# The first block's edges from the 49th on, held in the last block's tiles of a graph network

## The chip, the cores and the metric

The kernel runs on one core of one Trainium2 chip. The time is the device time of one execution in microseconds (us), and the smaller it is the better.

## The reference, cut to what matters

A graph has 6,250 nodes and 206,250 edges, sorted by their destination node; each node has an edge to itself, which stands last among its edges. The program is a two-part graph network.

```
h = relu(layernorm(x))
x = x + L0(h)                 # per edge: relu([h[dst], ea16] @ W1 + b1), mean over the edges of a node
h = relu(layernorm(x))
x = x + L1(h)                 # three attention layers, h -> h -> h
# one attention layer:
q, k, v = h @ Wq + bq, h @ Wk + bk, h @ Wv + bv
e       = ea32 @ We                                   # per edge
alpha   = sum(q[dst] * (k[src] + e)) / sqrt(C)        # per edge and head
a       = softmax of alpha over the edges of one dst
out     = sum over the edges of a * (v[src] + e), + h @ Ws + bs
```

Nodes have between 15 and 58 edges here, 33 on average. All floats are 32 bits wide.

## The kernel before, in words

**Blocks.** The nodes are sorted by their number of edges and cut into 49 blocks of 128, one node to a partition. Block 0 holds the 128 nodes with the most edges, block 48 the 106 with the fewest and 22 empty places. Block `b` has `CAP[b]` tiles: 66 for block 0, 46 for block 1, then fewer and fewer, 24 for block 47 and 22 for block 48; 1,661 in all. Tile `j` of a block holds the `j`-th edge of each of its 128 nodes. The last tile of a block is the edge of the node to itself; it needs no gather. So each attention layer gathers 1,661 - 49 = 1,612 tiles. In block 0 few nodes have more than 48 edges. There `lanes` cuts the gather of tile 48 to the first 64 partitions and that of tiles 49 to 64 to the first 32 (`CAP0`), and the rest of those chunks is zeroed on VectorE (L638).

**Before the layers (L97 to L383).** VectorE and TensorE count the edges of each node, put each node into a class by that number (`CLS` = 31 classes), rank the nodes (`oh`, `cnt`, `cum`, `at`: six VectorE operations over 31 x 49 columns, L275 to L292), and turn the rank into a block (`half[:, 0]`) and a partition (`half[:, 1]`). Checks on the input are summed into `bad`. `layer0` does L0 and gathers the source of each edge into `src[0]`, block by block. Then all engines branch (L397) on the sum of `bad`: at zero the three calls of `attention` follow, otherwise `general`, a path for any graph.

**One attention layer (`attention`).** The tiles of a block are held in chunks of `CT` = 8. `fetch(b)` issues on GpSimd's queue one indirect DMA per tile (`pick`, L447), which reads for each partition the key and value row of one source node from a table in HBM, `tab[l]`, into the tile's slot of a chunk `kv`. The chunks are a ring of 15 buffers in the first attention layer and of 18 in the other two. `load(b)` brings the edges' attributes on SyncE's queue. `process(b)` makes two passes over the chunks on VectorE. In the first, for each chunk, it adds the edge part that TensorE made (`pe`, L688, and L691 for the last tile), multiplies with `q` (L694) and sums (L695); in the first attention layer it also copies the source numbers out of the chunk (L687, a CAST), for the two later layers to use (`src[1]`). Then come the softmax (L701 to L712), with `lack` pushing absent edges down, and a second pass that weights (L717) and sums (L721) each chunk and sets its buffer free. At the end of a block its new rows go through TensorE and are written to the next layer's table (L738 to L740); the last layer instead keeps the block's result `hn` for a scatter on GpSimd's queue (`put`, L453).

**Order.** Blocks run from 0 to 48, with the gathers of a block issued while the one before it is processed:

```
load(0)
fetch(0)
for b in range(NB):
    if b + 1 < NB:
        load(b + 1)
        fetch(b + 1)
    put(b - 2)
    process(b)
put(NB - 2)
put(NB - 1)
```

Each queue runs in its own order. GpSimd's gathers stand in the order of the program. Within VectorE a scheduler mixes the instructions of neighbouring blocks at build time, and the chip runs them strictly in that order. A layer's first gather needs the whole table of the layer before it.

Of the kernel before, what the change touches and what calls it, by code (L numbers as in the profile page):

```python
# [22 lines left out]
F32 = mybir.dt.float32  # L23
# [4 lines left out]
OP = mybir.AluOpType  # L28
# [3 lines left out]
P = 128  # L32
N, E, D = 6250, 206250, 64
NB = 49
# [23 lines left out]
assert len(CAP) == len(LEAST) == NB  # L58
MAXC = max(CAP)

CAP0 = {64: 48, 32: 49}

LOW, HIGH = 20, (CAP0[64], CAP0[32])
CLS = HIGH[0] - LOW + 1 + len(HIGH)
LOOK = RUN + SG * (MAXC + 1) + 3
RMAX = (EP - LOOK) // RUN
assert CAP[1] < HIGH[0] and LEAST[-2] > LOW and RMAX * RUN + LOOK - 1 >= E
# [9 lines left out]

G = 4
NG = NCH // G


def lanes(b, j):

    return min([p for p in CAP0 if b == 0 and j >= CAP0[p]], default=P)


def runs(values):
# [10 lines left out]
def gnn_kernel(ctx: ExitStack, tc: tile.TileContext, x, src_t, dst_t, dst_row, ea16, ea32, eaT16, eaT32, w, out):  # L98
# [15 lines left out]
    with tc.tile_pool(name="chk", bufs=1) as p, tc.tile_pool(name="chk2", bufs=2) as p2, \  # L114
# [36 lines left out]
        def iota(n, mult, pattern=None):  # L151
# [14 lines left out]
        cap = p.tile([P, NB], F32, name="cap")  # L166
# [4 lines left out]
        nc.gpsimd.tensor_copy(cap, k.cap)  # L171
        nc.gpsimd.memset(cap[64:, 0:1], float(CAP0[64]))
        nc.gpsimd.memset(cap[32:64, 0:1], float(CAP0[32]))
# [94 lines left out]
        nc.vector.tensor_scalar(cls, deg, float(LOW), float(HIGH[0]), op0=OP.max, op1=OP.min)  # L268
        for h in HIGH:
            nc.vector.scalar_tensor_tensor(cls, deg, float(h), cls, op0=OP.is_gt, op1=OP.add)  # L270
        nc.vector.tensor_scalar(cls, cls, -float(LOW), float(CLS - 1), op0=OP.add, op1=OP.min)


# [23 lines left out]
        nc.vector.tensor_single_scalar(half_i[:, 1], int_i, P - 1, op=OP.bitwise_and)  # L297
        half = p.tile([P, 2, NB], F32, name="half")
        nc.vector.tensor_copy(half, half_i)
        pperm = pp.tile([P, 4, NB], F32, name="pperm", tag="pc")  # L300
        for b0 in range(0, NB, 7):
            to = p2.tile([P, 7, P], F16, name="to")
# [65 lines left out]
        nc.vector.tensor_tensor(no[:, 0], k.deg, cap, op=OP.is_gt)  # L368
        nc.vector.tensor_tensor(no[:, 1], k.deg, least, op=OP.is_lt)
        nc.vector.tensor_reduce(bad[:, 1:3], no, axis=AX.X, op=OP.add)  # L370
        for b in range(NB):
# [32 lines left out]
class Kept:  # L404
# [5 lines left out]
    def __enter__(self):  # L410
        self.stack = ExitStack()
        tc = self.tc
        cp = self.stack.enter_context(tc.tile_pool(name="kept", bufs=1))
        dr = self.stack.enter_context(tc.tile_pool(name="kdram", bufs=1, space=bass.MemoryType.DRAM))
        t = lambda name, shape, dt=F32: cp.tile([P] + shape, dt, name=name)

        self.num, self.deg, self.cap, self.ends = (t(n, [NB]) for n in ("num", "deg", "cap", "ends"))
        self.num_i, self.at_i = t("num_i", [NB], I32), t("at_i", [NB], I32)
        self.full = t("full", [WOFF[NB]])
        self.lack = t("lack", [WOFF[NB]])  # L420
        self.x1 = t("x1", [NB, D])
# [24 lines left out]
def pick(nc, out, table, idx):  # L446
    return nc.gpsimd.indirect_dma_start(out=out, out_offset=None, in_=table,  # L447
                                        in_offset=bass.IndirectOffsetOnAxis(ap=idx, axis=0))
# [12 lines left out]
def layer0(tc, ea16, ea32, ident, tabx, srcs, k):  # L461
    nc = tc.nc
    with tc.tile_pool(name="g0", bufs=4) as gp, tc.tile_pool(name="e0", bufs=2) as ep, \
# [124 lines left out]
        def put(b):  # L588
            scatter_rows(tc, k, k.tab[0][:, :], k.num_i[:, b:b + 1], k.rows[:, b, 2 * D:], NP - 1)
# [25 lines left out]
                    wait += [(r, b) for r in range(first[g], first[g] + FIN0[g])]  # L615
        for r, _ in wait:
            put(r)


def attention(tc, l, out, ident, slope, k):  # L620
# [5 lines left out]
    with tc.tile_pool(name=f"g{l + 1}", bufs=2) as gp, tc.tile_pool(name=f"e{l + 1}", bufs=3) as ep, \  # L626
# [7 lines left out]
        def fetch(b):  # L634
            for t0, n in chunks[b]:
                kv = kvs[b, t0] = ep.tile([P, CT, KV], F32, name="kv", bufs=15 if l == 0 else 18)
                if lanes(b, t0 + n - 1) < P:
                    nc.vector.memset(kv, 0.0)  # L638
                for j in range(n):
                    o = OFF[b] + t0 + j  # L640
                    if o + 1 < OFF[b + 1]:
                        r = lanes(b, t0 + j)
                        pick(nc, kv[:r, j, :], k.tab[l][:, :], idx[:r, o:o + 1])

        def load(b):
            g = slice(GOFF[b] * P, GOFF[b + 1] * P)
# [18 lines left out]
        def process(b):  # L665
# [12 lines left out]
            for t0, n in chunks[b]:  # L678
                kv = kvs[b, t0]
                pe = pp.tile([P, CT, D], F32, name="pe")  # L680
                for g in range(-(-n // 4)):
                    nc.tensor.matmul(pe[:, 4 * g:4 * g + 4].rearrange("p j f -> p (j f)"), ea[:, t0 // 4 + g, :],  # L682
                                     k.wblk[l], start=True, stop=True)
                m = n - (t0 + n == c)
                if m:
                    if l == 0:
                        nc.vector.tensor_copy(k.src[1][:, OFF[b] + t0:OFF[b] + t0 + m], kv[:, :m, 2 * D])  # L687
                    nc.vector.tensor_add(pair(kv[:, :m, :2 * D]), pair(kv[:, :m, :2 * D]),  # L688
                                         pe[:, :m, None, :].to_broadcast([P, m, 2, D]))
# [4 lines left out]
                nc.vector.tensor_mul(prod[:, :n], kv[:, :n, :D], q[:, None, :].to_broadcast([P, n, D]))  # L694
                nc.vector.tensor_reduce(al[:, :H, t0:t0 + n].rearrange("p h j -> p j h"),  # L695
                                        prod[:, :n].rearrange("p j (h c) -> p j h c", h=H), axis=AX.X, op=OP.add)
# [60 lines left out]
        put(NB - 2)  # L757
        put(NB - 1)


@with_exitstack
# [543 lines left out]
```

## Time and profile before

| | |
|---|---|
| time, median of 3 runs | 6730.41 us (6730.25 to 6735.94) |
| the profiled execution's own time | 6732.95 us |
| its span, first to last instruction | 6731.2 us |
| GpSimd (POOL) busy | 4927.7 us, 73% |
| VectorE (DVE) busy | 3127.9 us, 46% |
| TensorE (PE) busy | 1914.8 us, 28% |
| gathers of attention (L447, `kv<-tab,src`) | 4836, 943 ns each |
| first gather of the three attention layers | at 577.8, 2609.2 and 4639.6 us |

The trace gives each instruction's start and length. A row of a group reads: line, engine, operation, what it writes and reads, how many; then the busy time in us and the mean of one in ns; then the idle time of the engine just before those instructions and what ended it ("issue" where the profile shows no wait). A row of the timeline reads: start, length, engine, line, operation, and in brackets the idle time before it. For a DMA issued from GpSimd, the busy time is that of GpSimd, not that of the transfer.

### The profile page before, as it was taken

The page shows a single profiled execution, that of the slowest core. Times are in us where ns is not written, and L with a number is a line of the kernel's source. Part 1 is how long each engine was busy: PE and PEld are TensorE (multiplying, and loading weights), DVE is VectorE, ACT ScalarE, POOL GpSimd, SP SyncE. Part 2 cuts the span into 40 slices and gives each one's busy share as a digit, 9 for nine tenths or more (in the row PEclk, how much of TensorE's full clock was granted, in tenths as well). Part 3 has the DMA queues.
Part 4 walks back from the last instruction along what each step waited for, and adds up shares of the span by engine and source line. Part 5 has one row for each costly group of instructions (what it writes and reads, how often), then busy time and mean ns, then how long its engine had stood idle before and what let it go on. Part 6 is the DMA issues. An engine that isn't in the chain of part 4 may idle for free. (4 is left out here: it accounts for less than half of the span.)

```text
span 6731.2 us, 26890 instructions
## 1 busy us (share of the span) xinstructions
PE 1914.8 (28%) x4808; PEld 1135.6 (17%) x4808; DVE 3127.9 (46%) x5986; ACT 345.5 (5%) x998; POOL 4927.7 (73%) x5264
## 2 busy tenths in 40 slices
PE   4663232333333332222222222222222222222221
PEld 3442111111111111111111111111111111111110
DVE  7763444444444444444444444444444344444444
ACT  3110000000000000000000000000000000000000
POOL 4556777777777776777777777776777777777776
PEclk9765555555555555555555555555555555555555
DMA  4553232333232322222222222222222222222221
GB/s 144 183 175 122 81 87 79 84 84 84 82 87 81 84 82 60 67 69 66 68 69 68 68 70 67 69 68 64 64 63 68 63 66 66 66 64 67 63 65 55
DMA packets 227799, 535.37 MB, mean 80 GB/s; under 512 B 90199, under 2 KB 106685, under 8 KB 226519
## 3 DMA queue, kind: packets, MB, share of 16 engines
q0 software_dynamic: 172736, 374.78, 19.6%
q1 hardware_dynamic: 52790, 156.27, 7.0%
q10 hardware_dynamic: 2090, 2.48, 0.1%
q14 instruction: 142, 1.16, 0.1%
q8 instruction: 41, 0.67, 0.0%
HBM read 459.32 MB, written 73.87 MB: 79 GB/s over the span
## 5 line engine op out<-in xcount | busy, mean ns | idle before, releaser
L447 POOL DMA_INDIRECT kv<-tab,src x4836 | 4561.7, 943 | 1518.6 <-issue 1410.4
L688 DVE TENSOR_TENSOR kv<-kv,pe 128x1024 f32<-128x1024 f32 (+6 forms) x669 | 745.0, 1114 | 2321.1 <-DMA kv<-tab,src 2152.6
L682 PE MATMUL pe<-wblk,ea 128*128 128x256 f32 x1736 | 901.4, 669 | 3046.8 <-DVE kv L688 2747.1
L682 PEld LDWEIGHTS pe<-wblk,ea 128*128 128x128 f32 x1736 | 505.7, 323 | 3420.6 <-DVE kv L688 2967.0
L682 PE MATMUL pe<-wblk,eaT 128*128 128x256 f32 x868 | 451.4, 668 | 1224.9 <-DVE kv L688 1160.8
L721 DVE TENSOR_REDUCE some<-kv 128x64 f32<-128x512 f32 (+6 forms) x690 | 610.6, 922 | 0.1
L687 DVE CAST src<-kv 128x8 int32<-128x8 f32 (+5 forms) x223 | 41.0, 184 | 1092.5 <-DMA kv<-tab,src 1041.6
L682 PEld LDWEIGHTS pe<-wblk,eaT 128*128 128x128 f32 x868 | 252.1, 322 | 1383.1 <-DVE kv L688 1273.3
L694 DVE TENSOR_TENSOR prod<-kv,more 128x512 f32<-128x512 f32 (+6 forms) x690 | 423.7, 628 | 0.8
L695 DVE TENSOR_REDUCE al<-prod 128x16 f32<-128x512 f32 (+8 forms) x690 | 422.9, 627 | 0.7
L717 DVE TENSOR_TENSOR kv<-kv,more 128x512 f32<-128x512 f32 (+6 forms) x690 | 416.7, 627 | 0.0
L706 ACT ACTIVATE more<-al,m 128x33 f32<-128x33 f32 (+22 forms) x245 | 71.7, 293 | 3189.0 <-DVE m L704 3185.8
L518 PE MATMUL pm<-w0blk,eT 64*128 64x256 f32 x868 | 192.2, 564 | 37.0 <-DVE msg L521 20.0
L659 PE MATMUL turn<-ident,ea 128*128 128x128 f32 x434 | 124.9, 432 | 77.5 <-ACT eaT L660 70.8
L453 POOL DMA_INDIRECT tab<-rows,num_i x49 | 54.5, 1112 | 117.5 <-ACT rows L586 97.9
L539 DVE TENSOR_TENSOR msg<-msg 128x960 f32<-128x960 f32 (+19 forms) x224 | 137.4, 617 | 0.8
L518 PEld LDWEIGHTS pm<-w0blk,eT 64*128 64x128 f32 x868 | 120.3, 276 | 89.6 <-DVE msg L521 25.7
L521 DVE TENSOR_TENSOR msg<-pm,rx 128x1024 f32<-128x1024 f32 x76 | 92.8, 1221 | 77.4 <-PE pm L518 72.0
L447 POOL DMA_INDIRECT e<-in_ea_dram,at_i x98 | 103.8, 1059 | 33.8 <-issue 22.2
L738 PE MATMUL po<-ws,ht 65*128 65x256 f32 x196 | 109.2, 661 | 11.5 <-ACT ht L736 11.5
L674 ACT COPY more<-rows 128x64 f32<-128x64 f32 x147 | 31.6, 216 | 1516.3 <-DVE kv L717 1507.9
L659 PEld LDWEIGHTS turn<-ident,ea 128*128 128x128 f32 x434 | 80.2, 217 | 139.1 <-ACT eaT L660 125.9
(183 smaller groups left out, 1442.8 us busy)
## 6 DMA issues: line engine op xcount, KB each, us to landing
kv<-tab,src POOLq DMA_INDIRECT x4836, 2.5
ea<-eat SPq DMA_DIRECT2D x26, 576.0 KB
ea<-eat SPq DMA_DIRECT2D x24, 512.0 KB
ea<-eat SPq DMA_DIRECT2D x16, 640.0 KB
ean<-e SPq DMA_DIRECT2D x13, 576.0 KB
ea<-ean SPq DMA_DIRECT2D x13, 576.0 KB
eat<-eaT SPq DMA_DIRECT2D x13, 576.0 KB
ea<-eat SPq DMA_DIRECT2D x16, 448.0 KB
```

The source lines that it names most:

```text
L447: return nc.gpsimd.indirect_dma_start(out=out, out_offset=None, in_=table, in_offset=bass.IndirectOffsetOnAxis(ap=idx, axis=0))
L518: nc.tensor.matmul(pm[:, r, u].rearrange("p j f -> p (j f)"), eT[h, t0 // 8 + u, :], k.w0blk[h, :], start=True, stop=True)
L521: nc.vector.tensor_tensor(msg[:, t0:t0 + 16], pm.rearrange("p r u j f -> p (r u j) f"), nega[:, None, :].to_broadcast([P, 16, D]), op=OP.max)
L539: nc.vector.tensor_add(to, msg[:, :h], msg[:, c - h:c])
L659: nc.tensor.transpose(ps[:, i - i0, :], t[:, i, :], ident)
L682: nc.tensor.matmul(pe[:, 4 * g:4 * g + 4].rearrange("p j f -> p (j f)"), ea[:, t0 // 4 + g, :], k.wblk[l], start=True, stop=True)
L688: nc.vector.tensor_add(pair(kv[:, :m, :2 * D]), pair(kv[:, :m, :2 * D]), pe[:, :m, None, :].to_broadcast([P, m, 2, D]))
L694: nc.vector.tensor_mul(prod[:, :n], kv[:, :n, :D], q[:, None, :].to_broadcast([P, n, D]))
L695: nc.vector.tensor_reduce(al[:, :H, t0:t0 + n].rearrange("p h j -> p j h"), prod[:, :n].rearrange("p j (h c) -> p j h c", h=H), axis=AX.X, ...
L717: nc.vector.tensor_mul(v.rearrange("p j (h c) -> p j h c", h=H), v.rearrange("p j (h c) -> p j h c", h=H), ex[:, :H, t0:t0 + n].rearrange( ...
L721: nc.vector.tensor_reduce(some[:, i, :], v.rearrange("p j f -> p f j"), axis=AX.X, op=OP.add)
L738: nc.tensor.matmul(po, ht[:, :P], k.ws[l + 1], start=True, stop=True)
```

## The change

Block 0 keeps gathers for its own tiles 0 to 48 only (`OWN0` = 49). What a node of block 0 has beyond 49 edges is put into places of block 48's tiles that its node there does not use: tile `t` of block 0, from 49 to 64, lies in tile 69 - `t` of block 48 (`SHARE`). For this the nodes of block 48 stand in reverse order on the partitions (`turned`), so that the nodes with the most edges in block 0 meet the empty places and the nodes with the fewest edges in block 48. `share` writes the source numbers of those edges into block 48's part of `src[0]` once, after `layer0`. In `process(0)` the addition of the edge part reads these rows out of block 48's chunks, in reverse order of tiles, and writes them into block 0's own chunks. Block 48's tiles must then be there when block 0 is processed: the two come first in `order`, and block 47 is the last.

The classes become 33 (one for empty places, and the two above 49 in place of 48 and 49), a check that each pair of nodes fits is added to `bad`, and `lanes`, the zeroing of chunks and the tile `cap` go.

```diff
-CAP0 = {64: 48, 32: 49}
-LOW, HIGH = 20, (CAP0[64], CAP0[32])
-CLS = HIGH[0] - LOW + 1 + len(HIGH)
+OWN0 = 49
+SHARE = OWN0 + CAP[-1] - 2
+NOVER = CAP[0] - 1 - OWN0
+LOW, HIGH = 20, (OWN0, OWN0 + 1)
+CLS = HIGH[0] - LOW + 2 + len(HIGH)
...
+        nc.vector.scalar_tensor_tensor(cls, deg, 0.0, cls, op0=OP.is_gt, op1=OP.add)
...
+        turned = p.tile([P, NB], F32, name="turned")
+        nc.vector.tensor_scalar(turned, half[:, 1], -2.0, float(P - 1), op0=OP.mult, op1=OP.add)
+        nc.vector.scalar_tensor_tensor(turned, half[:, 0], float(NB - 1), turned, op0=OP.is_equal, op1=OP.mult)
+        nc.vector.tensor_add(half[:, 1], half[:, 1], turned)
...
+        over = p.tile([P, 2], F32, name="over")
...
+        nc.vector.tensor_scalar(k.over, col[:, OWN0:CAP[0] - 1], k.deg[:, 0:1], None, op0=OP.is_lt)
...
+def share(nc, k):
+    a = k.src[0][:, OFF[0] + OWN0:OFF[0] + CAP[0] - 1]
+    b = k.src[0][:, OFF[NB - 1]:OFF[NB]][:, SHARE - OWN0:SHARE - (CAP[0] - 1):-1]
+    d = k.shared
+    nc.vector.tensor_sub(d, a, b)
+    nc.vector.tensor_mul(d, d, k.over)
+    nc.vector.tensor_add(b, b, d)
...
         def fetch(b):
             for t0, n in chunks[b]:
                 kv = kvs[b, t0] = ep.tile([P, CT, KV], F32, name="kv", bufs=15 if l == 0 else 18)
-                if lanes(b, t0 + n - 1) < P:
-                    nc.vector.memset(kv, 0.0)
-                for j in range(n):
+                for j in range(own_tiles(b, t0, n)):
                     o = OFF[b] + t0 + j
-                    if o + 1 < OFF[b + 1]:
-                        r = lanes(b, t0 + j)
-                        pick(nc, kv[:r, j, :], k.tab[l][:, :], idx[:r, o:o + 1])
+                    pick(nc, kv[:, j, :], k.tab[l][:, :], idx[:, o:o + 1])
+
+        def own_tiles(b, t0, n):
+            return max(0, min(n, (OWN0 if b == 0 else CAP[b] - 1) - t0))
+
+        def shared(t0, n):
+            out, t = [], max(t0, OWN0)
+            while t < min(t0 + n, CAP[0] - 1):
+                c, i = divmod(SHARE - t, CT)
+                u = min(t0 + n, CAP[0] - 1, t + i + 1)
+                out.append((t - t0, u - t0, kvs[NB - 1, c * CT][:, i - (u - t) + 1:i + 1, :2 * D][:, ::-1]))
+                t = u
+            return out
...
-                m = n - (t0 + n == c)
+                m = own_tiles(b, t0, n)
...
-                if m < n:
-                    nc.vector.tensor_add(pair(kv[:, m:n, :2 * D]), pair(own[:, None, 2 * D:4 * D]),
-                                         pe[:, m:n, None, :].to_broadcast([P, 1, 2, D]))
+                for i, j, rows in shared(t0, n) if b == 0 else []:
+                    nc.vector.tensor_add(pair(kv[:, i:j, :2 * D]), pair(rows),
+                                         pe[:, i:j, None, :].to_broadcast([P, j - i, 2, D]))
+                if t0 + n == c:
+                    nc.vector.tensor_add(pair(kv[:, n - 1:n, :2 * D]), pair(own[:, None, 2 * D:4 * D]),
+                                         pe[:, n - 1:n, None, :].to_broadcast([P, 1, 2, D]))
...
-        load(0)
-        fetch(0)
-        for b in range(NB):
-            if b + 1 < NB:
-                load(b + 1)
-                fetch(b + 1)
-            put(b - 2)
+        order = [0, NB - 1] + list(range(1, NB - 1))
+        for b in order[:2]:
+            load(b)
+            fetch(b)
+        for i, b in enumerate(order):
+            if i and i + 1 < NB:
+                load(order[i + 1])
+            if i and i + 1 < NB:
+                fetch(order[i + 1])
+            if i > 1:
+                put(order[i - 2])
             process(b)
-        put(NB - 2)
-        put(NB - 1)
+        put(order[-2])
+        put(order[-1])
```

More of the change, by code (lines that the diff above doesn't have):

```diff
@@ L79 @@
 NG = NCH // G
-def lanes(b, j):
-    return min([p for p in CAP0 if b == 0 and j >= CAP0[p]], default=P)
 def runs(values):
@@ L165, in gnn_kernel @@
                                 pattern=[[1, P]], channel_multiplier=-1)
-        cap = p.tile([P, NB], F32, name="cap")
         least = p.tile([P, NB], F32, name="least")
@@ L170, in gnn_kernel @@
                 nc.gpsimd.memset(t[:, i:j], float(v))
-        nc.gpsimd.tensor_copy(cap, k.cap)
-        nc.gpsimd.memset(cap[64:, 0:1], float(CAP0[64]))
-        nc.gpsimd.memset(cap[32:64, 0:1], float(CAP0[32]))
         going = p.tile([P, CLS, NB], BF16, name="going")
@@ L367, in gnn_kernel @@
         no = p.tile([P, 2, NB], F32, name="no")
-        nc.vector.tensor_tensor(no[:, 0], k.deg, cap, op=OP.is_gt)
+        nc.vector.tensor_tensor(no[:, 0], k.deg, k.cap, op=OP.is_gt)
         nc.vector.tensor_tensor(no[:, 1], k.deg, least, op=OP.is_lt)
         nc.vector.tensor_reduce(bad[:, 1:3], no, axis=AX.X, op=OP.add)
+        over = p.tile([P, 2], F32, name="over")
+        nc.vector.tensor_scalar(over[:, 0:1], k.deg[:, 0:1], float(CAP[0] - 1), -float(OWN0), op0=OP.min, op1=OP.add)
+        nc.vector.tensor_scalar(over[:, 1:2], k.deg[:, NB - 1:], float(CAP[-1] - 1), None, op0=OP.min)
+        nc.vector.tensor_add(over[:, 1:2], over[:, 1:2], over[:, 0:1])
+        nc.vector.tensor_scalar(over[:, 1:2], over[:, 1:2], float(CAP[-1] - 1), None, op0=OP.is_gt)
+        nc.vector.scalar_tensor_tensor(bad[:, 4:5], over[:, 0:1], 0.0, over[:, 1:2], op0=OP.is_gt, op1=OP.mult)
+        nc.vector.tensor_scalar(k.over, col[:, OWN0:CAP[0] - 1], k.deg[:, 0:1], None, op0=OP.is_lt)
         for b in range(NB):
@@ L420, in __enter__ @@
         self.lack = t("lack", [WOFF[NB]])
+        self.over = t("over", [NOVER])
+        self.shared = t("shared", [NOVER])
         self.x1 = t("x1", [NB, D])
@@ L617, in layer0 @@
             put(r)
+        share(nc, k)
+def share(nc, k):
[5 more added lines that the diff above has]
+    nc.vector.tensor_add(b, b, d)
 def attention(tc, l, out, ident, slope, k):
```

## The prediction

> **What bounds the kernel now.** I read the page first, then the groups, then GpSimd's waits and its timeline over 577 to 720 us and around the two changes of layer, then VectorE's timeline there.
>
> ```profile
> PE 1914.8 (28%) x4808; PEld 1135.6 (17%) x4808; DVE 3127.9 (46%) x5986; ACT 345.5 (5%) x998; POOL 4927.7 (73%) x5264
> L447 POOL DMA_INDIRECT kv<-tab,src x4836 | 4561.7, 943 | 1518.6 <-issue 1410.4
> POOL kv L447 <- issue: 1410.4, 4481, 20.4
> ```
>
> In the first two rows GpSimd's gathers are 4561.7 us busy and 1518.6 us idle just before them: 6080 of the span's 6731 us. The idle time is put down to "issue", that is to no wait that shows. The chain of waits on the page says nothing here (it stops at the last scatter), so the bound is read from the timeline:
>
> ```profile
> 635.27 0.94 POOL L447 DMA_INDIRECT kv<-tab,src  x1 [0.30 <-issue]
> 636.52 0.94 POOL L447 DMA_INDIRECT kv<-tab,src  x1 [0.30 <-issue]
> 637.77 0.92 POOL L447 DMA_INDIRECT kv<-tab,src  x1 [0.30 <-issue]
> 638.99 0.89 POOL L447 DMA_INDIRECT kv<-tab,src  x1 [0.30 <-issue]
> 640.19 0.87 POOL L447 DMA_INDIRECT kv<-tab,src  x1 [0.30 <-issue]
> ...
> 656.66 0.87 POOL L447 DMA_INDIRECT kv<-tab,src  x1 [0.30 <-issue]
> 657.83 0.95 POOL L447 DMA_INDIRECT kv<-tab,src  x1 [0.30 <-issue]
> ```
>
> One gather starts every 1.25 us (0.94 busy, 0.30 between), and no gap is longer inside a layer. The rows from 637.77 to 656.66 are tiles 48 to 64 of block 0: with 32 partitions a gather still takes 0.87 + 0.30 = 1.17 us. So the length of a layer is the number of its gathers, and rows left out of a gather hardly shorten it. Only a layer's end is not gathers:
>
> ```profile
> 2587.80 0.94 POOL L447 DMA_INDIRECT kv<-tab,src  x1 [0.30 <-issue]
> 2609.15 0.94 POOL L447 DMA_INDIRECT kv<-tab,src  x1 [20.40 <-issue]
> 2593.57 0.16 DVE L687 CAST src<-kv 128x5 int32<-128x5 f32 x1
> 2593.64 0.81 DVE L688 TENSOR_TENSOR kv<-kv,pe 128x640 f32<-128x640 f32 x1
> 4615.77 1.22 DVE L688 TENSOR_TENSOR kv<-kv,pe 128x1024 f32<-128x1024 f32 x1 [5.36 <-DMA kv<-tab,src]
> 4624.48 0.81 DVE L688 TENSOR_TENSOR kv<-kv,pe 128x640 f32<-128x640 f32 x1
> 4639.55 0.94 POOL L447 DMA_INDIRECT kv<-tab,src  x1 [19.32 <-issue]
> 6711.85 0.94 POOL L447 DMA_INDIRECT kv<-tab,src  x1 [0.30 <-issue]
> 6716.32 0.82 DVE L688 TENSOR_TENSOR kv<-kv,pe 128x640 f32<-128x640 f32 x1
> 6717.58 0.56 DVE L694 TENSOR_TENSOR prod<-kv,more 128x384 f32<-128x384 f32 x1
> ```
>
> These are the ends of the attention layers 1, 2 and 3. GpSimd waits there some 20 us for VectorE to finish the last block and for the table to be written. Call G the start of the layer's last gather (2587.80, 4619.28, 6711.85). VectorE adds the edge part to the last chunk at G + 5.8, G + 5.2 and G + 4.5.
>
> **The change, part by part.**
>
> *Gathers.* Per layer, block 0's tiles 48 to 64 took from 637.77 to 657.83 = 20.06 us. Tile 48 stays, with 128 partitions: 1.25 us. Sixteen gathers go: 18.8 us a layer, **56.4 us** in three. A rule of the Trainium skill speaks against this. DMA: Bandwidth & Descriptors, section "Anatomy of one DMA — SWDGE (gpsimd) path", fits such a DMA by 2.0 us plus its bytes at 436 GB/s, says that the fixed part is nearly all completion latency, and calls making descriptors small. Latency of transfers in flight together is hidden, so by that rule a removed gather of 32 rows of 512 bytes would give back its 16 KB, 0.04 us by an estimate, and 48 of them 1.8 us. The rows above show another price: 1.17 us of GpSimd's own queue, one after the other. The trace's duration is used.
>
> *Setup.* The six operations over 31 classes took 1.74 + 1.73 + 3.91 + 2.11 + 1.98 + 2.79 = 14.26 us on VectorE (L275 to L292); at 33 classes 2/31 more, 0.92. One more operation on `cls` and three for `turned` start some 0.12 apart, as their like do: 0.48. VectorE runs there with hardly a gap and the last layernorm groups stand behind it, so **+1.4**. The six small ones of the fit check and `k.over` (0.7) stand behind that chain, ahead only of the 41 `full` operations and `lack`, which end 1.5 us before the first gather of `layer0` has its other inputs: 0. The GpSimd copy and two memsets that go were not on a path: 0.
>
> *share.* Three operations on 16 columns, some 0.5 us. Block 48's sources are in at 567.5; the next VectorE instruction in line, the loop check, starts at 573.57, after an idle 10.15 us that a transfer to `ean` ends. Covered by 6 us. Without cover: 0.5.
>
> *Start of a layer.* Block 0's last three chunks now wait for the 70th gather, not the 65th, and block 1's gathers follow. What could stop GpSimd is the ring. In layer 1, with 15 buffers (9 chunks of block 0, 3 of block 48, 3 of block 1), the fourth chunk of block 1 needs block 0's first one free, 25 gathers after the 70th: 31 us. In the built program's order VectorE has, after the 70th lands (2.7 us): the last addition, block 48's first pass, block 0's remaining products, softmax, and two weighted chunks: four additions (1.14, 1.14, 0.72, 0.4), some eight products and sums of 0.6, the small ones 1.5, and 3 for the second pass: about 13 us. Free at 16 us, needed at 31. With 18 buffers it is needed after 56 us. The six additions with reversed tiles are not in the trace: from below, what they replace; from above, twice the plain rate, 16 tiles x 0.14 = 2.2 us more. I take the lower end plus three starts of 0.2 us, since a reversed operand in the trace (L286) runs no slower than its neighbours. All of it lies under the 15 us: 0. The three zeroings of 0.94 us that go were under gathers too: 0. SyncE's loads and GpSimd's scatters keep their lead of one block.
>
> *End of a layer.* Last is now block 47, whose last chunk has 8 tiles, 7 gathered, against 6 and 5. That costs VectorE 0.28 in the addition, 0.12 each in product, sum and weighting, 0.05 in the last sum, less 0.12 for L708 that block 48 alone needs: +0.55 a layer. More depends on where the scheduler put block 46's second pass, and that is to be seen in the order of the built program. For layer 1 VectorE's order there is:
>
> ```
> 2585 L718 TensorCopy src1<-kv 128x7            the CAST of the last chunk
> 2586 L744 TensorReduce s<-more 128x2           block 46's second pass
> ...
> 2599 L719 TensorTensor kv<-kv,pe 128x7x128     the last chunk's addition
> ```
>
> The work between is counted from one start to the next in the trace: a wide addition 1.14, products and weightings 0.6, sums of the second pass 0.92, small ones 0.07 to 0.3.
> - Layer 1: the CAST that waits for the last gather now stands ahead of the whole pass. It starts at G + 2.75 at the earliest, then 6.1 us of pass come before the addition: G + 8.9 against G + 5.84, so +3.1.
> - Layer 2: the chunk before the last lands at G - 8.74 + 2.73 (4615.77 less its gather's 4613.04 is 2.73). From there 8.5 us of work end at G + 2.5, and the last chunk lands at G + 2.75: against G + 5.2, so -2.45.
> - Layer 3: the addition stands ahead of the pass, at G + 2.7. Then 1.0 for itself and 7.1 for the pass, block 46's end and the second chunk's product and sum bring the last product to G + 10.8, against 6717.58 = G + 5.73: +5.1. In GpSimd's order one scatter (1.3 us) moves from before G to behind it, where GpSimd waits anyway: -1.3.
>
> The ends together: 3.1 - 2.45 + 5.1 - 1.3 + 3 x 0.55 = **+6.1**.
>
> *Sum.* -56.4 + 1.4 + 6.1 = -48.9. The profiled execution took 6732.95 us: 6684.0. It lies 2.5 above the median of the three runs, which spread over 5.7; I predict **6683 us**.
>
> **The rivals.**
> 1. The ends cost nothing: the pass finds its place under the landing, as in layer 2. Then -56.4 + 1.4: 6677 on the median. For it: layer 2's order. Against it: an engine runs in its order, and two of three orders are the other way. 7%.
> 2. The ring. If VectorE frees block 0's first chunk in layer 1 not 16 but more than 31 us after the 70th gather, GpSimd stands still with block 1's fourth chunk, and all later gathers move with it. Each us beyond 31 is lost. At 80 us the gain of 48.9 is gone, at 95 the kernel is 15 us slower, 6745. Needed for that is something that holds block 0 for 65 us, say block 48's gathers or edge attributes coming late behind SyncE's queue. For it: block 0 now depends on two blocks. Against it: the attributes are loaded before both, and no gap inside a layer shows today. 3%.
> 3. The rule above holds, and the time of a gather comes from what is in flight: -1.8 + 1.4 + 6.1 on the median, 6736. Against it are the 17 rows at 1.17. 1%.
> 4. The change does not do what it says: if one pair of nodes does not fit, all goes through `general`, whose gathers alone, 404 x 4 in each of three layers at 1.25 us, are 6.05 ms, after a start of 0.58 ms. Counted from the reference's inputs, 19 nodes have over 50 edges and seven have 50. The first 22 of these 26 meet the 22 empty places, with at most 58 - 49 = 9 edges to hold; the last four bring one edge each to nodes of at most 20, in 21 places. It fits. 1%.
>
> **How the numbers follow.** The forecast has 88%. Its range holds 4 us for the ends (another place of the pass in each), 2 for setup, 5 for the spread of the runs. Rival 1 lies inside. Range 6672 to 6698; it leaves out rivals 2 to 4 and a tenth of the forecast. A measurement can tell some 0.2%, 13 us, from no change. Faster: the forecast and rival 1, with a little off for a stall in part, 0.95. Same: rival 3 and part of rival 2, 0.02. Slower: 0.03.
>
> **What would show it.** 4788 gathers at L457 with none at 0.87; one every 1.25 us with no gap over 0.4 inside a layer; some 1991 us from a layer's first to its last gather (2587.80 - 577.77 less 18.8); the gaps at the two changes of layer near 24 and 17.5 us; the first attention gather 1 to 2 us later. Wrong would be a gap in block 1's fourth chunk, or GpSimd's idle share growing by what its busy time lost.

## The result, and the profile after

| | before | after |
|---|---|---|
| time, median of 4 runs | 6731.16 us (6730.25 to 6735.94) | 6693.44 us (6691.98 to 6694.64) |
| the profiled execution's own time | 6732.95 us | 6694.13 us |
| its span | 6731.2 us | 6692.4 us |

The ratio is 0.9941, with a 95% interval of 0.9929 to 0.9954: the changed kernel is faster by 37.7 us. The forecast of 6683 us is 10.4 us too low, and its range holds the result.

The rows of the page that answer to those shown of before: busy time of the engines, the gathers of attention (now at L457), and GpSimd's waits ahead of them (us in total, times, longest).

```profile
PE 1909.7 (29%) x4808; PEld 1133.7 (17%) x4808; DVE 3119.5 (47%) x5997; ACT 345.5 (5%) x998; POOL 4882.0 (73%) x5213
L457 POOL DMA_INDIRECT kv<-tab,src x4788 | 4520.5, 944 | 1505.9 <-issue 1402.9
POOL kv L457 <- issue: 1402.9, 4450, 24.1
```

GpSimd's gathers have lost 41.2 us of busy time and 12.7 us of the idle time between them; their share of the span is still nine tenths. The view by tile has their shortest, median and longest:

```profile
L457 POOL DMA_INDIRECT kv<-tab,src x4788: 938/944/1062, 581.4 to 6660.5; - x200
```

4788 gathers, none at 870 ns any more. The timeline at the ends of layers 1, 2 and 3 (start, length, engine, line, operation, and the idle time before it):

```profile
2573.08 0.94 POOL L457 DMA_INDIRECT kv<-tab,src  x1 [0.30 <-issue]
2598.11 0.94 POOL L457 DMA_INDIRECT kv<-tab,src  x1 [24.09 <-issue]
2575.69 0.17 DVE L718 CAST src<-kv 128x7 int32<-128x7 f32 x1 [6.81 <-DMA kv<-tab,src]
2575.77 0.20 DVE L744 TENSOR_REDUCE s<-more 128x2 f32<-128x50 f32 x1
2582.00 1.07 DVE L719 TENSOR_TENSOR kv<-kv,pe 128x896 f32<-128x896 f32 x1
...
4589.21 0.94 POOL L457 DMA_INDIRECT kv<-tab,src  x1 [0.30 <-issue]
4592.03 1.09 DVE L719 TENSOR_TENSOR kv<-kv,pe 128x896 f32<-128x896 f32 x1
4607.71 0.94 POOL L457 DMA_INDIRECT kv<-tab,src  x1 [17.56 <-issue]
...
6660.49 0.94 POOL L457 DMA_INDIRECT kv<-tab,src  x1 [0.30 <-issue]
6663.31 1.09 DVE L719 TENSOR_TENSOR kv<-kv,pe 128x896 f32<-128x896 f32 x1 [7.49 <-DMA kv<-tab,src]
6671.54 0.68 DVE L728 TENSOR_TENSOR prod<-kv,more 128x512 f32<-128x512 f32 x1
```

G is again the start of a layer's last gather (2573.08, 4589.21 and 6660.49). In layer 1 the CAST waits for the last gather and the whole second pass of block 46 follows it, so the last chunk's addition comes at G + 8.92. In layer 2 it comes at G + 2.82, in layer 3 at G + 2.82, with the last product at G + 11.05.

The two executions laid side by side, in stretches that follow on each other (here G is that of layer 3, and L is the start of the last scatter):

| stretch | before, us | after, us | difference | predicted |
|---|---|---|---|---|
| start to the first attention gather | 577.78 | 581.39 | +3.6 | +1.4 |
| layer 1, to the first gather of layer 2 | 2031.4 | 2016.7 | -14.7 | -15.15 |
| layer 2, to the first gather of layer 3 | 2030.4 | 2009.6 | -20.8 | -20.7 |
| layer 3, to G | 2072.3 | 2052.8 | -19.5 | -20.1 |
| G to L | 13.8 | 19.5 | +5.7 | +5.65 |
| L to the end of the span | 5.5 | 12.4 | +6.9 | 0 |
| sum | | | -38.8 | -48.9 |

The three layers and their ends came out within 1.0 us of the forecast in all. What is missing lies at the two ends of the kernel: 2.2 us ahead of attention, and 6.9 us behind the last scatter. For the last stretch, the timeline of GpSimd has nothing after the scatter:

```profile
6671.90 0.98 POOL L463 DMA_INDIRECT out_dram<-hn,num_i  x1 [7.83 <-DVE hn L776]
6679.99 0.98 POOL L463 DMA_INDIRECT out_dram<-hn,num_i  x1 [7.12 <-POOLq L405]
```

The scatter is issued by 6680.97, but the span ends at 6692.4. The raw records behind this view, which list the instructions that count as no work, name what stands there: a DRAIN on GpSimd's queue that starts at 6682.7 and takes 8869 ns. In the kernel before, the same instruction starts at 6728.3 and takes 952 ns. It is 7.9 us longer after the change; 1.2 us of that come back in the few records behind it, which leaves the 6.9 of the table.

### The profile page after: what moved, and what is told of

The parts are those of the page before. It is cut to its first block, busy times and chain, and to the rows that moved or that the text cites. A ratio compares the mean times of both kernels' runs of the same rounds, so it can differ in the third digit from the quotient of the medians.

```text
span 6692.4 us, 26810 instructions
## 1 busy us (share of the span) xinstructions
PE 1909.7 (29%) x4808; PEld 1133.7 (17%) x4808; DVE 3119.5 (47%) x5997; ACT 345.5 (5%) x998; POOL 4882.0 (73%) x5213
## 5 line engine op out<-in xcount | busy, mean ns | idle before, releaser
L457 POOL DMA_INDIRECT kv<-tab,src x4788 | 4520.5, 944 | 1505.9 <-issue 1402.9
L729 DVE TENSOR_REDUCE al<-prod 128x16 f32<-128x512 f32 (+10 forms) x690 | 423.2, 628 | 0.6
L457 POOL DMA_INDIRECT e<-in_ea_dram,at_i x98 | 102.5, 1046 | 37.5 <-issue 22.0
L772 PE MATMUL po<-ws,ht 65*128 65x256 f32 x196 | 108.8, 659 | 10.4 <-ACT ht L770 10.4
```

The source lines that it names most:

```text
L772: nc.tensor.matmul(po, ht[:, :P], k.ws[l + 1], start=True, stop=True)
```

## The experiments

My theory: every gather costs its own turn on GpSimd's queue, whatever its rows; the ends of layers follow VectorE's fixed order. The rivals: the time of a gather is its latency and bytes; the ends are set by something else. Later came the two misses: is the long DRAIN the kernel's own or chance, and what makes attention start late? The experiments ran on three chips, on which the kernel before takes 7708.79 us (e1 to e4), 7687.54 us (e5 to e8) and 6746.68 us (e9 to e12), so each time is set against that of its own chip ("ratio" is always the ratio to the kernel before there, with its 95% interval); on the first two VectorE waits long ahead of the addition of the edge part, and GpSimd then stands still inside the layers for want of a free chunk.

**e1_order: the order of the blocks alone.** The kernel before, with

```diff
-        for b in range(NB):
+        order = [0, NB - 1] + list(range(1, NB - 1))
```

and the loop of the changed kernel over it.

> The kernel before with the block order of the change alone (0, 48, 1 to 47); the gathers with 64 and 32 partitions stay. Theory A (the sum of the prediction: only the ends of the layers move): gaps between the layers near 24.1 and 17.6 us, one scatter from before the last gather to behind it, the last scatter 5.7 us later after the last gather; in all +3.1 - 2.45 + 5.1 - 1.3 + 1.65 = +6 us over before. Theory B1 (the 6.9 us that came on top behind the last scatter belong to the order, since the last scatter is now of a block with 128 rows in range): GpSimd's drain at the end is near 8.9 us here too, and the time is +13. Theory B2 (they belong to the number of gathers): the drain stays near 1 us, and the time is +6.

Measured: 7722.38 us, ratio 1.0015 (1.0008 to 1.0021), so 6 to 16 us more. The order alone costs time, as the ends in the forecast (+6.1) had it. Its size is not settled: the median, 13.6 us more, is nearer to the +13 of theory B1, and the layers' ends cannot be read one by one, since GpSimd has gaps everywhere on this chip. B1 itself is out: GpSimd's DRAIN took 946 ns, so neither the new order nor the new last block makes it long.

**e2_end_47_43: another end.** The changed kernel, with

```diff
-        order = [0, NB - 1] + list(range(1, NB - 1))
+        order = [0, NB - 1] + [b for b in range(1, NB - 1) if b not in (43, 47)] + [47, 43]
```

> The change with the blocks in the order 0, 48, 1 to 46 without 43, then 47, 43. In the built program the addition of the last chunk now stands behind the second pass of the block before in all three layers, and the last chunk has 3 tiles, 2 gathered, in place of 8 and 7. Counting VectorE's work from the last gather as in the prediction, the ends come some 6.5, 0.5 and 7.2 us sooner than in the change: gaps near 17.6 and 17 us, the last scatter near 12.3 us after the last gather instead of 19.5. Theory A (order within VectorE sets the ends): 14 us less than the change, about 6679 us. Rival (the ends are set by the table writes and the projection, not by where the addition stands): within 3 us of the change. If the drain behind the last scatter belongs to a last block with 128 rows, it stays near 8.9 us.

Measured: 7658.53 us, ratio to the kernel before 0.9932 (0.9918 to 0.9945). By itself it settles nothing, since the changed kernel did not run beside it; it was run again as e6 and e12. The DRAIN took 8877 ns.

**e3_two_rows: the gathers put back, with 2 rows each.** The changed kernel, and in each attention layer 16 gathers of two rows into the slots of block 0 that the addition then writes over; nothing uses them.

```diff
+                for j in range(n):
+                    o = OFF[b] + t0 + j
+                    if b == 0 and OWN0 <= t0 + j < CAP[0] - 1:
+                        pick(nc, kv[:2, j, :], k.tab[l][:, :], k.src[0][:2, o:o + 1])
```

> The change with the 16 gathers of block 0 put back in each layer, each for two partitions only (2 rows of 512 bytes); the additions overwrite what they bring, so they are ballast. Theory A (a gather costs its place in GpSimd's queue, whatever it moves): 48 gathers at 1.10 to 1.17 us, +53 to +56 us over the change, about 6748 us. Rival, the fit by fixed completion latency and bytes: 1 KB each, nothing that a measurement can tell, within 3 us of the change. For the drain at the end: if it goes with the number of gathers it changes from 8.9 us, if with the last scatter it stays.

Measured: 7729.97 us, ratio to the kernel before 1.0027 (1.002 to 1.0035). The gain is gone, though almost no bytes have come back. Its timeline of GpSimd at block 0's tiles, from the first gathers of two rows to the first of 128 rows behind them:

```profile
694.60 0.88 POOL L457 DMA_INDIRECT kv<-tab,src  x1 [0.30 <-issue]
695.79 0.87 POOL L457 DMA_INDIRECT kv<-tab,src  x1 [0.31 <-issue]
...
712.02 0.86 POOL L457 DMA_INDIRECT kv<-tab,src  x1 [0.30 <-issue]
713.18 0.97 POOL L457 DMA_INDIRECT kv<-tab,src  x1 [0.30 <-issue]
```

Sixteen gathers of two rows take 713.18 - 694.60 = 18.6 us, or 1.16 each; with 32 rows it was 1.17, with 128 it is 1.25. That is the price per instruction of GpSimd's queue, and the rows hardly enter it. The DRAIN took 9369 ns, with as many gathers as the kernel before has.

**e4_setup: the new setup alone.** The changed kernel up to the branch (classes, `turned`, the check of the pairs, `share`), with `fetch`, the additions and the order of the kernel before.

> The setup of the change (33 classes, the turned partitions, the fit check, the writing of the shared sources) with the attention layers of before, whose gathers with 64 and 32 partitions stay. Prediction: +1.4 us over before, all of it ahead of the first gather of attention. What the profiles of before and of the change show: that gather came 3.6 us later, with the stage of L0 4.3 us longer and the part before it 0.7 us shorter. If that is the setup's own, the first gather of attention stands at 581.4 here and the time is +3.6; if it is the scatter of single executions (the clock granted to TensorE was 0.50 from 100 to 130 us in one and 1.00 in the other), the first gather stands anywhere between 576 and 583 and the time is within 2 us of before. The drain at the end: near 1 us if it goes with the order or the number of gathers.

Measured: 7711.53 us, ratio 1.0000 (0.9991 to 1.0008). The interval reaches from -7 to +6 us, too wide to size a few microseconds. Its trace says more. The first gather of `layer0` comes at 122.67 us, and at 123.44, 123.9 and 124.04 in the three traces with the old setup (before, e1, e7): the setup is not longer but some 1 us shorter. Then, between the 37th and the 43rd of GpSimd's DMAs counted from the start, it falls back by 5.4 us against e7 (by 5.0 against e1, which ran on the same chip). Every trace with the new setup has this step, 4.3 to 9.0 us, but for the two at the end of this section that take certain copies off ScalarE; e1, with the old setup, has 0.4. The DRAIN took 946 ns: not the setup.

**e5_after: the changed kernel again.**

> The changed kernel itself, so that the next three stand beside it on one chip. By its first runs 0.9941 of the kernel before. The two things that the prediction had not: if GpSimd's DRAIN at the very end of 8.9 us (0.95 in the kernel before) belongs to the kernel, it is there again (8.8 to 9.0); if it was chance, it is near 1. If the 4.3 us that layer0's stage had gained belonged to the TensorE clock of that one execution (0.50 granted over 100 to 130 us, against 1.00), they are gone where the clock is granted in full there, and the first attention gather comes not over 1.5 us later than in the kernel before on the same chip; if the change itself costs them (more on VectorE ahead of layer0), they are there again.

Measured: 7637.53 us, ratio 0.9942 (0.9928 to 0.9955), the same gain in per cent. The DRAIN took 8868 ns: it belongs to the kernel. The TensorE clock was granted at 0.50 over 100 to 120 us here too, and at 1.00 in e2, which has the step as well: the clock is not what makes attention late.

**e6_end_47_43: the other end beside it.** The edit of e2.

> The changed kernel with blocks 47 and 43 as the last two of the order, and nothing else changed. My theory is that the end of a layer is decided by VectorE's fixed order: counted from that order, VectorE's last product of the three layers comes at G + 11.0, 10.8 and 10.8 us (G: the start of the layer's last gather) where the changed kernel has 17.5, 11.3 and 17.9 in the same count: 14 us less than e5_after, a ratio to it of 0.998. The gaps between the layers would be near 17.6 and 17.1 us. Rival: something else sets the gaps (the landing of the last gather, TensorE, the write of the table), and the order of the blocks alone moves nothing: the same as e5_after within 3 us, gaps near 24 and 17.5.

Measured: 7651.3 us, ratio to the kernel before 0.9952 (0.9939 to 0.9966), and no gain over e5: 13.8 us more, with its five runs spread over 24.6 us and overlapping those of e5. That is not what the theory gives, but it is no test of it either. GpSimd's waits in e5:

```profile
POOL kv L457 <- issue: 1576.7, 4627, 58.8
POOL kv L457 <- DVE some L755: 531.7, 40, 24.9
```

In 40 places, 532 us in all, GpSimd waits for VectorE to free a chunk, and the gap between layers is up to 58.8 us. VectorE is a whole ring of chunks behind there, so what stands last in its order after G need not set the end. The question was left for a chip on which it keeps up (e12).

**e7_wide_tile48: 64 rows more, in the kernel before.**

```diff
-                        r = lanes(b, t0 + j)
+                        r = P if b == 0 and t0 + j == 48 else lanes(b, t0 + j)
```

> The kernel before, with one number changed: tile 48 of block 0 is gathered on all 128 partitions in place of 64 (64 rows more in each attention layer, as many gathers as before). For the time of a gather: 3 x 0.1 us or less, the ratio to the kernel before is 1.000. For GpSimd's DRAIN at the end: if its length goes with how many rows the gathers have moved in all[...], it is no longer 0.95 us but another, most likely near 8.9; if it goes with the code of the changed kernel (its length, or what the last instructions are), it stays at 0.95.

Measured: 7688.23 us, ratio 0.9998 (0.9989 to 1.0006): 192 rows more cost nothing that this measurement can tell, within some 8 us. The DRAIN took 1028 ns, still short.

**e8_28_rows: the gathers put back, with 28 rows each.** The edit of e3 with `kv[:28, j, :]` and 28 sources.

> The changed kernel with 16 gathers of 28 rows each put back into every attention layer, into the slots of block 0 that the addition of the edge part then writes over; nothing uses them. Rows in all: 16 x 28 = 448, as many as the kernel before has more than the changed one (16 x 32 - 64). For the time, by the price of a gather on GpSimd's queue (1.17 us at 32 rows): 48 x 1.17 = 56 us over e5_after, +0.8%; by the fixed part hidden in flight[...]: under 2 us. For GpSimd's DRAIN at the end: if it goes with the rows in all, it is 0.95 us again as in the kernel before; if it goes with the code of the changed kernel or with the number of gathers, 8.8 to 9.4 as in the changed kernel.

Measured: 7699.75 us, ratio to the kernel before 1.0022 (1.0013 to 1.0031), so 62.2 us over e5, where the price of a gather gave 56. Part of it is given back by the DRAIN, which fell to 1039 ns; the rest, 62.2 + 7.8 - 56 = 14 us, is for the most part more standing still on this chip: GpSimd's idle stretches of over 1 us from the end of `layer0` on sum to 760 us in its trace and to 748 in that of e5. Why they grew was not followed up. For the DRAIN this is the clearest pair: e3 and e8 differ only in the rows of 48 gathers. All kernels together, by how many rows more or fewer than the kernel before the attention layers gather:

| kernels | rows | gathers | DRAIN at the end, ns |
|---|---|---|---|
| before, e1, e4 | 0 | 4836 | 952, 946, 946 |
| e7 | +192 | 4836 | 1028 |
| e8 | 0 | 4836 | 1039 |
| e3 | -1248 | 4836 | 9369 |
| after, e2, e5, e6, e9, e10, e11, e12 | -1344 | 4788 | 8868 to 8883 |

So in these 14 traces its length goes with how many rows the gathers have moved in all, not with the number of gathers, the order of the blocks or the new code. Why a smaller sum makes it longer, and where the border lies between -1248 and 0, stays open; so does whether it is the sum itself or where the sum leaves off in something that fills up and starts over, since no kernel tells the two apart.

**e9_after: the changed kernel, as the base of the next three.**

> The changed kernel once more, as the base of the next three on one chip: 0.994 of the kernel before. In layer0's stage ScalarE's fixed order holds, in the changed kernel alone, a copy of the last edge's source (the CAST into ends, which waits for a gather to land) between the two copies of the fourth block's eT; I expect the second of those two (128x256) to start some 6 us after the first (128x512) here too, and TensorE's products pm behind it as late.

Measured: 6705.22 us, ratio 0.9942 (0.9928 to 0.9955). Here VectorE keeps up, as in the first traces. The step in `layer0` is there (5.6 us against the first trace of the kernel before). ScalarE's timeline around it, first in the kernel before, then in the changed one (its first trace; e9's is the same within 1.5 us):

```profile
159.11 0.19 ACT L490 CAST ends<-src 128x1 f32<-128x1 int32 x1 [4.90 <-DMA src<-srcs,at_i]
159.21 0.85 ACT L509 COPY eT<-turn 128x512 f32<-128x512 f32 x2
167.18 0.19 ACT L490 CAST ends<-src 128x1 f32<-128x1 int32 x1 [7.11 <-DMA src<-srcs,at_i]
171.90 0.19 ACT L490 CAST ends<-src 128x1 f32<-128x1 int32 x1 [4.53 <-DMA src<-srcs,at_i]
171.99 0.85 ACT L509 COPY eT<-turn 128x512 f32<-128x512 f32 x2
```

```profile
160.38 0.19 ACT L500 CAST ends<-src 128x1 f32<-128x1 int32 x1 [6.19 <-DMA src<-srcs,at_i]
160.48 0.58 ACT L519 COPY eT<-turn 128x512 f32<-128x512 f32 x1
166.40 0.19 ACT L500 CAST ends<-src 128x1 f32<-128x1 int32 x1 [5.34 <-DMA src<-srcs,at_i]
166.49 0.36 ACT L519 COPY eT<-turn 128x256 f32<-128x256 f32 x1
171.52 0.19 ACT L500 CAST ends<-src 128x1 f32<-128x1 int32 x1 [4.66 <-DMA src<-srcs,at_i]
176.92 0.19 ACT L500 CAST ends<-src 128x1 f32<-128x1 int32 x1 [5.21 <-DMA src<-srcs,at_i]
177.02 0.85 ACT L519 COPY eT<-turn 128x512 f32<-128x512 f32 x2
```

Each CAST takes a block's last source number out of a gather (`ends`, for the check of the loops) and waits for that gather to land; the copies of `eT` behind it feed TensorE. Two things differ. A CAST stands between the two copies of the fifth block (the text on record counts it from 0), and three CASTs, not two, stand ahead of the sixth block's pair, which comes at 177.02 and not at 171.99. The first order is also that of e1 and e7, which have the old setup; the second is that of every kernel with the new setup but e10, e11 and e12.

**e10_cast_two_blocks_later: no CAST between the two copies.** The changed kernel with

```diff
-            nc.scalar.copy(k.ends[:, b:b + 1], k.src[0][:, OFF[b + 1] - 1:OFF[b + 1]])
...
+        def last(b):
+            nc.scalar.copy(k.ends[:, b:b + 1], k.src[0][:, OFF[b + 1] - 1:OFF[b + 1]])
...
                 load_src(b)
+                if b > 1:
+                    last(b - 2)
```

> The changed kernel with the CAST of a block given to the scheduler two blocks later in the program; its order on ScalarE then is that of the kernel before at the fourth block (both copies of eT together, then the CAST), and nearly the same elsewhere. My theory: the split pair is what makes the first attention gather late, and it comes 4 to 5 us earlier than in e9_after (5 less in all, 0.9993 of it). Rival: layer0's stage is set by something else (the six more operations of setup, the TensorE clock), and the first attention gather stays within 1.5 us of e9_after's.

Measured: 6706.63 us, ratio to the kernel before 0.9943 (0.9929 to 0.9956), the same as e9. The first attention gather comes 4.0 us earlier than in e9's trace but 0.5 later than in the first trace of the changed kernel, so this shows no gain. Nor can the time of a whole run show 4 us: in e10's trace layer 1 takes 1995.4 us from its first gather to its last, in e9's 1991.3, with the same 1,596 gathers (1.251 us each for 1.248), so e9's profiled run is the shorter one in the end. ScalarE's timeline shows what did not change:

```profile
159.24 0.85 ACT L521 COPY eT<-turn 128x512 f32<-128x512 f32 x2
166.68 0.19 ACT L502 CAST ends<-src 128x1 f32<-128x1 int32 x1 [6.59 <-DMA src<-srcs,at_i]
171.53 0.19 ACT L502 CAST ends<-src 128x1 f32<-128x1 int32 x1 [4.65 <-DMA src<-srcs,at_i]
177.68 0.19 ACT L502 CAST ends<-src 128x1 f32<-128x1 int32 x1 [5.96 <-DMA src<-srcs,at_i]
177.78 0.85 ACT L521 COPY eT<-turn 128x512 f32<-128x512 f32 x2
```

The two copies stand together, but still three CASTs stand ahead of the next pair. My theory of the split pair falls, for the step in `layer0` is there without it (4.3 us against the first trace of the kernel before); what is left is the third CAST.

**e11_cast_on_gpsimd: no CAST on ScalarE at all.** e10 with `nc.gpsimd.tensor_copy` in `last`.

> The changed kernel with all 49 CASTs of ends moved from ScalarE to GpSimd, each behind the source gather of two blocks later. ScalarE waits 196.1 us in 41 places for those landings in the changed kernel's trace, GpSimd is busy for 263 of the stage's 458 us. If ScalarE's waits are on the path of layer0 in most blocks, the first attention gather comes 30 to 80 us earlier than in e9_after; if they lie under the gathers of edges and TensorE's products, it comes 5 us earlier, as in e10, or up to 15 later (49 x 0.3 us more on GpSimd's queue).

Measured: 6691.6 us, ratio to the kernel before 0.9919 (0.9905 to 0.9932). That is 13.6 us less than e9 and 15.0 less than e10, with no overlap of the runs. The first attention gather comes at 568.67 us, against 581.39, 581.85 and 585.86 in the traces of after, e10 and e9. The trace of e10 is the one to compare with, since its gathers start as far apart (1.251 us): 13.2 us earlier there, and 13.8 us less in the time of that run. The sixth block's pair of copies, at 177.02 us in the changed kernel, comes at 160.58 (the first line of ScalarE's timeline below) and the seventh's, there at 182.16, at 166.23; the step is gone:

```profile
160.58 0.86 ACT L521 COPY eT<-turn 128x512 f32<-128x512 f32 x2 [8.49 <-PE pm L530]
166.23 0.76 ACT L521 COPY eT<-turn 128x512 f32<-128x512 f32 x2 [4.78 <-PE turn L520]
```

So the CASTs on ScalarE hold up `layer0`, though only a small part of the 205.3 us that ScalarE waits for them in e9 lies on the path; the expected 30 to 80 us was too much. A kernel that takes away only the third CAST, and not the other 48, was not tried, so its share is seen in the traces and not measured alone; nor was it compared whether the build moved other instructions too.

**e12_both: e11 with the end of e2.**

> e11 with blocks 47 and 43 as the last two of the order. It takes what the CASTs give before the first attention gather, and, by VectorE's order, G + 11.0, 10.8 and 10.8 us for the last products of the three layers (the changed kernel: 17.5, 11.3, 17.9), 14 us less in all where VectorE keeps up with the gathers (no gap of GpSimd inside a layer). Where it does not keep up, as in e6_end_47_43, the ends are set by what VectorE is behind, and the order of the last blocks gives nothing: the same as e11 within 15 us.

Measured: 6677.32 us, ratio to the kernel before 0.9896 (0.9881 to 0.9911), and 14.3 us less than e11; the slowest run of e12, 6679.81, lies below the fastest of e11, 6690.95. The first lines below are e11's timeline, the second those of e12 (the gaps of GpSimd between the layers, then the last scatter):

```profile
2588.78 0.95 POOL L457 DMA_INDIRECT kv<-tab,src  x1 [23.93 <-issue]
4602.30 0.95 POOL L457 DMA_INDIRECT kv<-tab,src  x1 [17.44 <-issue]
6658.58 0.95 POOL L457 DMA_INDIRECT kv<-tab,src  x1 [0.30 <-issue]
6678.14 0.97 POOL L463 DMA_INDIRECT out_dram<-hn,num_i  x1 [7.13 <-POOLq L405]
```

```profile
2581.37 0.95 POOL L457 DMA_INDIRECT kv<-tab,src  x1 [17.46 <-issue]
4594.43 0.95 POOL L457 DMA_INDIRECT kv<-tab,src  x1 [16.93 <-issue]
6652.12 0.95 POOL L457 DMA_INDIRECT kv<-tab,src  x1 [0.30 <-issue]
6664.31 0.97 POOL L463 DMA_INDIRECT out_dram<-hn,num_i  x1 [8.32 <-POOLq L405]
```

The gaps shrink by 6.5 and 0.5 us, and the way from G to the last scatter from 19.56 to 12.19, by 7.4: together 14.3. VectorE's order, counted in the built program, gave 6.5, 0.5 and 7.2 (in the words of the expectation, the count is of the last product; what it counts is the end of VectorE's work for the layer). The rival, by which the order of the blocks moves nothing, is out where VectorE keeps up. e12 beats the kernel before by 69 us and the changed one by 28.

## Why the prediction was right or wrong

**Gathers: right.** Forecast were 16 a layer at 1.17 us (less what the wider tile 48 costs), 18.8; from a layer's first to its last gather the traces have 2010.0, 2010.1 and 2072.3 before and 1991.7, 1991.1 and 2052.8 after: 18.3, 19.0 and 19.5 us less, the last with the one scatter (1.3 us) that moved behind G, so 18.2 for the gathers alone. e3 shows that it is the instruction and not its bytes that costs. The rule weighed there, with 2.0 us of hidden latency plus bytes (the Trainium skill, DMA: Bandwidth & Descriptors, section "Anatomy of one DMA — SWDGE (gpsimd) path"), gave 1.8 us for all 48 by an estimate; it describes how long one transfer takes to land (2.5 us in the median of this trace, where an estimate by the rule gives 2.15 for 64 KB), and this case is bound by how fast they are issued.

**Ends of layers: right.** The four terms added up to the gaps of 24 and 17.5 us that the trace has (24.09 and 17.56), and to +5.65 for the way to the last scatter (+5.7). The lines shown of after have the last addition at G + 8.92 where the forecast said G + 8.9, and the last product at G + 11.05 for G + 10.8. e12 against e11 shows that it is what VectorE has in line behind G that sets them.

**Start of a layer and the ring: right.** No gap between gathers inside a layer is over 0.32 us in the trace of after. In block 0 VectorE does wait for block 48's gathers, 55.5 us in 6 places, but under the gathers that follow. The additions with reversed tiles (five a layer; the sixth that the text on record counts is tile 48's own) run like their neighbours, as taken (groups by shape, busy us and mean ns; L722 is the reversed one):

```profile
L719 DVE TENSOR_TENSOR kv<-kv,pe 128x768 f32<-128x768 f32 x18 | 17.1, 951 | 28.6 <-DMA kv<-tab,src 24.0 <-issue 4.6
L722 DVE TENSOR_TENSOR kv<-kv,pe 128x768 f32<-128x768 f32 x3 | 2.9, 955 | 35.7 <-DMA kv<-tab,src 35.7
```

**Setup: the term was mis-sized, and its mechanism was wrong.** I took the operations that were added one by one and put +1.4 on the path. The setup itself ended 0.7 us earlier (first gather of `layer0` 122.73 for 123.44). The six operations over the classes took 14.30 us for 14.26, so the 2/31 more did not show. VectorE's order also came out differently behind them, and it waits 1.7 us less for TensorE's product `pperm` (the first line is of the kernel before, the second of the changed one):

```profile
95.94 1.09 DVE L303 TENSOR_TENSOR to<-iota,half 128x896 f16<-128x896 f32 x1 [2.60 <-PE pperm L312]
94.81 1.09 DVE L303 TENSOR_TENSOR to<-iota,half 128x896 f16<-128x896 f32 x1 [0.90 <-PE pperm L312]
```

What the time went to was a side effect that I had not looked for, since I compared the orders of VectorE and GpSimd only: ScalarE's order in `layer0` came out with one more wait ahead of the sixth block's `eT`. Together +3.6 in place of +1.4, in this one pair of traces: the changed kernel's own two traces have the first attention gather at 581.39 and 585.86, so the size is known to a few us only. What does not hang on one trace is the step: 4.3 to 9.0 us in every trace that has both the new setup and the CASTs on ScalarE, 0.4 at most in the others. e4 puts it down to the setup; that it is the third CAST fits the traces and e11, but is not shown alone.

**The end of the kernel: a term that was missing.** "In GpSimd's order one scatter moves from before G to behind it" was the whole account of the end, and it held. That a DRAIN behind the last scatter could change from 0.95 to 8.87 us was in no view that I had read. With what follows it, it is 6.9 of the 10.1 us by which the sum was off. That the range held the result is in part luck: its allowances were for the ends, the setup and the spread of the runs, the DRAIN was none of them, and the ends came out so close that their share was free to cover it.

**Slips in the sums, on which nothing hangs.** Rival 1 comes to 6675 on the median (6730.41 - 55.0), not 6677, and the forecast itself to 6681.5 on the median; 6683 lies between that and the 6684.0 of the profiled execution.

## What to carry to other kernels

Where a queue issues its indirect gathers one after the other without a gap, count instructions, not rows: a gather of 2 rows cost 1.16 us and one of 128 rows 1.25. After a change that renumbers or adds operations early, compare the static order of every engine, also of those that it does not touch: here a tiny copy that waits for a landing moved in front of what feeds TensorE, and a step of 4.3 us or more went with it, where all that was added had been put at 1.4. And where the engine keeps up, the stage's end is set by what the fixed order puts behind the last landing: choosing which two blocks come last was worth 14 us of 6692.

## What the runs showed of the hardware

GpSimd's DRAIN behind the last scatter took 0.95 to 1.04 us or 8.87 to 9.37 us, by the rows that the gathers had moved in all, and much the same in each trace of a kernel (8868 to 8883 ns in the eight traces with the rows of the changed one). The page shows it only as time between the last scatter and the end of the span.

The kernel before took 6731, 7709, 7688 and 6747 us in the four series of runs. In the traces of all four a gather starts as soon after the one before it (1.249 to 1.252 us in the median); in the second and third VectorE waits up to 42.9 us ahead of an addition of the edge part, for something that the profile calls "remote" (no such wait stands there in the other two), and the ring of chunks stays full so long. What that is was not found. The changed kernel ran in three of the four, and gave the same 0.6% each time: 0.9941, 0.9942 and 0.9942.
